# Attention scores and P @ v in causal blocks of 64 keys, on halves of the TensorE array

## The chip, the cores and the metric

The kernel runs on one core of a Trainium2 chip. The metric is the device time of one execution in microseconds (us). All data is float32.

## The reference, cut to what matters

```
x: [8, 256, 512]                                   # 8 sequences of 256 tokens
h = layernorm(x)
qkv = h @ w_qkv                                    # 32 q heads, 8 k and v heads, 128 wide
scores = q @ k.T * 128 ** -0.5                     # 4 q heads share a k and v head
scores += -slope[head] * sqrt(q_pos - k_pos)       # -inf where k_pos > q_pos
attn = softmax(scores);  o = attn @ v
x = x + o @ w_o
h = layernorm(x)
hits = softmax(h @ centroids.T / 0.1) > 0.01       # 64 clusters
dense = h @ weight.T + bias
x = x + where(any(hits, 1)[:, None] & any(hits, 0)[assignments], dense, 0)
```

## The kernel before

The eight sequences are taken in four pairs of two. A **unit** `u` is one k and v head with its four q heads, on one sequence: 8 heads x 8 sequences = 64 units, in order of pair, head, sequence. `slot` is the unit's number within its pair, 0 to 15; even units are the first sequence of a head, odd ones the second. The loop runs two units further to finish what is left.

Scores stand transposed: keys on the partitions, queries along the columns. With keys 0 to 127 all 256 queries are computed, with keys 128 to 255 the upper 128 queries only, so a unit has 4 x 256 + 4 x 128 = 1536 columns. What of them lies above the diagonal is masked by the bias (`dist` holds 3e38 there).

Several units are in work at once. In unit `u` these steps are issued, by an order written out by hand, each engine taking its own in that order:

- `scores(u, 0)` and `(u, 1)` (L376, two heads each) and, after a part of the projections, `(u, 2)` (L382, the second block of keys). VectorE multiplies and adds the bias (L378, L384).
- `over_keys(s[u], ..., max)`: VectorE's transposing reduces (L393 over 1024 columns, L394 over 512), and one small combine where both blocks hold the same queries (L396).
- `subtract_max(u - 1)`: GpSimd on the first block (L428), VectorE on the second (L431); then ScalarE's exp (L765).
- `attend(u - 2)`, named `av(0)` and `av(1)` in the order, for heads 0 and 1, then 2 and 3: TensorE's P @ v (L452, L453, into one bank of `p_acc`), VectorE's multiplication by 1 / sum into `oT` (L456). Then GpSimd's sums S1 to S4 of `oT` (L112 to L118).
- `over_keys(s[u - 1], ..., add)`, `over_quadrants`: TensorE transposes the reduced rows `r` (L403), VectorE reduces them (L407), and the result goes by DMA to HBM (L412) and back to all partitions (L421, `bc`): the maxima of `u` and 1 / sum of `u - 1`.
- `project_out(u - 2)`, steps named `w(1)` to `w(7)` (L474): product 1 reads `oT` of the first token tile, and begins with heads 0 and 1.
- the projections for later units: q (`qq`) in every unit, v (`e`) in slots 0, 1, 8, 9, k (`e`) in slots 3, 7, 11, 15 (L145), and the FFN (`f`) in slots 3 to 6 of the second and third pair.

All projections are by a scheme of seven products of quarter matrices (`strassen`), with sums of the weights on GpSimd or VectorE (`a_sums`: S1 to S4). In slots 0 and 8 VectorE makes S3 and S4 of the v weights after `subtract_max`.

TensorE's results lie in PSUM pools: `p_sc` has two banks, `p_acc` three; a new tile waits until the reader of an older one has released its bank. All loads stand on SP's queue. Before the loop, a warm-up has matmuls of `ones` on the whole array (L625), on halves of its rows (L628) and on halves of its columns (L631). Near the end, L933 and L938 compute the mask of the output columns; L938 uses 64 rows of the array.

The order of an even unit with a k or v projection:

```
qq(1), e(1), max_and_old(), e(2), f(0), av(0), e(6), exp_old(), av(1), more_sums(), f(1), rows_max(), f(1.5), e(7), qq(2)
```

and of an odd one:

```
e(1), qq(4), e(2), max_and_old(), f(0), e(6), av(0), exp_old(), e(7), av(1), f(1), f(1.5), e(5), qq(5)
f(2), norm(0), e(4), e(3), x(0), w(1), x(1), sum_old(), w(2, 5, 6), norm(1), qq(3)
```

Of the kernel before, what the change touches and what calls it, by code (L numbers as in the profile page):

```python
# [23 lines left out]
G = NH // NKV  # L24
# [11 lines left out]
X2_BUFS = 8  # L36

# [6 lines left out]
def sqrt_distances():  # L44


    k = np.arange(P)[:, None]
    q = np.arange(S)[None, :]
    d = np.where(q >= k, np.sqrt(np.maximum(q - k, 0).astype(np.float32)), np.float32(MASKED))
    return np.ascontiguousarray(d.astype(np.float32))  # L50
# [3 lines left out]
def block_kernel(  # L54
# [31 lines left out]
    alibi_hbm = [dram.tile([P, G * S], F32, tag=f"al_hbm{kv}", name=f"al_hbm{kv}", bufs=1) for kv in range(NKV)]  # L86
# [90 lines left out]
    def load_x2(t):  # L177
        x2[t] = work.tile([P, H], F32, tag="x2", name=f"x2_{t}", bufs=X2_BUFS)
        nc.sync.dma_start(x2[t], xf[ts(t, P), :])
# [69 lines left out]
    dist_sb = const.tile([P, S], F32, name="dist_sb")  # L249
# [97 lines left out]
    def alibi_bias(g):  # L347

        p, kv = divmod(g, NKV)
        t = bias_sb[g] = work.tile([P, G, S], F32, tag="alibi", name="alibi", bufs=2)  # L350
        if p == 0:
            for h in range(G):
                nc.gpsimd.tensor_scalar(t[:, h, :], dist_sb, -slopes[kv * G + h], None, ALU.mult)
            nc.sync.dma_start(alibi_hbm[kv], t.rearrange("p h q -> p (h q)"))
        else:
            nc.sync.dma_start(t.rearrange("p h q -> p (h q)"), alibi_hbm[kv])
# [3 lines left out]
    K0, K1 = G * S, G * P  # L360
    J0, J1 = K0 // 32, K1 // 32
    s_sb, inv_sb, bc_sb = {}, {}, {}

    def scores(u, i):
# [5 lines left out]
        if i == 0:  # L370
            s_sb[u] = work.tile([P, K0 + K1], F32, tag="s", name="s", bufs=3)
        s = s_sb[u]
        sc = p_sc.tile([P, 512], F32, tag="sc", name="sc")
        if i < 2:
            hh = 2 * i
            nc.tensor.matmul(sc, lhsT=kT[:, t0 : t0 + P], rhs=qT[:, hh : hh + 2, t0 : t0 + S],  # L376
                             start=True, stop=True)
            nc.vector.scalar_tensor_tensor(  # L378
                s[:, hh * S : (hh + 2) * S], sc, D ** -0.5,
                bias[:, hh : hh + 2, :].rearrange("p h q -> p (h q)"), ALU.mult, ALU.add)  # L380
        else:
            nc.tensor.matmul(sc, lhsT=kT[:, t0 + P : t0 + S], rhs=qT[:, :, t0 + P : t0 + S],  # L382
                             start=True, stop=True)
            nc.vector.scalar_tensor_tensor(  # L384
                s[:, K0:].rearrange("p (h q) -> p h q", h=G), sc.rearrange("p (h q) -> p h q", h=G),
                D ** -0.5, bias[:, :, :P], ALU.mult, ALU.add)

    def over_keys(s, r, which, op):  # L390
        a, b = which * J0, 2 * J0 + which * J1
        first, second = r[:, a : a + J0], r[:, b : b + J1]
        nc.vector.tensor_reduce(first, s[:, :K0].rearrange("p (j q) -> p j q", q=32), AX.X, op, apply_transpose=True)  # L393
        nc.vector.tensor_reduce(second, s[:, K0:].rearrange("p (j q) -> p j q", q=32), AX.X, op, apply_transpose=True)  # L394
        late = first.rearrange("p (h i) -> p h i", h=G)[:, :, 4:8]
        nc.vector.tensor_tensor(late, late, second.rearrange("p (h i) -> p h i", h=G), op)  # L396

    def over_quadrants(u, r, has_max, has_sum):

# [5 lines left out]
        for on, a, op in ((has_max, 0, ALU.max), (has_sum, J0, ALU.add)):  # L405
            if on:
                nc.vector.tensor_reduce(row[a : a + J0], tp[a : a + J0, :P].rearrange("j (c q) -> j q c", q=32),  # L407
                                        AX.X, op)
# [3 lines left out]
        nc.sync.dma_start(hbm[lo:hi], row[lo:hi])  # L412
        for on, i in ((has_max, 0), (has_sum, 1)):
            if on:

                if i == 0 or u == 0:
                    bc_sb[u] = work.tile([P, 2, G, S], F32, tag="bc", name="bc")
                to = bc_sb[min(u, NU - 1)][:, i if u < NU else 0]
                if i == 1:
                    inv_sb[u - 1] = to  # L420
                nc.sync.dma_start(to.rearrange("p h q -> p (h q)"),  # L421
                                  hbm[ts(i, J0)].rearrange("j q -> (j q)").partition_broadcast(P))

    def subtract_max(u, i):
        s, mx = s_sb[u], bc_sb[u][:, 0]
        if i == 0:
            k0 = s[:, :K0].rearrange("p (h q) -> p h q", h=G)
            gp(k0, k0, mx, sub)  # L428
        else:
            k1 = s[:, K0:].rearrange("p (h q) -> p h q", h=G)  # L430
            ve(k1, k1, mx[:, :, P:], sub)  # L431

    o_sb = {}

    def attend(u, e):
# [5 lines left out]
        i0 = bb * 2  # L441
        pT, inv = s_sb[u], inv_sb[u]
        if e == 0:
# [4 lines left out]
        oT = o_sb[u][0]  # L448
        hh = 2 * e
        av = p_acc.tile([P, 512], F32, tag="acc", name="av")  # L450
        av3 = av.rearrange("p (h q) -> p h q", h=2)
        nc.tensor.matmul(av, lhsT=v[:, i0, vc], rhs=pT[:, hh * S : (hh + 2) * S], start=True, stop=False)  # L452
        nc.tensor.matmul(av3[:, :, P:S], lhsT=v[:, i0 + 1, vc],  # L453
                         rhs=pT[:, K0 + hh * P : K0 + (hh + 2) * P].rearrange("p (h q) -> p h q", h=2),
                         start=False, stop=True)
# [552 lines left out]
```

## Time and profile before

| | |
|---|---|
| time, median of 3 runs | 1411.86 us (1409.46 to 1412.16) |
| the profiled execution | 1410.37 us, of which the profile's span is 1408.5 us |
| matmul records in it | 5875 |
| DMA over the span | 190.20 MB, mean 135 GB/s |

PE is TensorE's matmuls, PEld its weight loads, DVE VectorE, ACT ScalarE, POOL GpSimd, SP the engine whose queue issues the loads. Durations of one record and starts are from the profiled execution. A float32 matmul is two records, one per pass over the columns. A record's length goes on after the next has started, so a step is counted from start to start. In a row, `64*128` or `128*64` after the operation are the rows and columns of the array that it uses.

### The profile page before, as it was taken

What the parts mean: (1) busy time and instruction counts of PE and PEld (TensorE: products, weight loads), DVE (VectorE), ACT (ScalarE), POOL (GpSimd) and SP (SyncE); (2) the same over time, 40 slices, a digit from 0 to 9 for tenths busy, and PEclk for the clock granted to TensorE, in tenths of its full rate; (3) what the DMA queues carried; (4) which work ended last, traced back from release to release, by engine and by line L of the source; (5) the groups of instructions that cost most, each with busy time, mean ns of one, the idle gap of its engine ahead of it and who ended that gap; (6) DMA issues with size and microseconds to landing.
All of it is one profiled execution on the core that took longest, in us unless ns stands there. A gap on an engine that the chain in (4) does not pass through costs nothing.

```text
span 1408.5 us, 16598 instructions
## 1 busy us (share of the span) xinstructions
PE 1394.1 (99%) x5875; PEld 1085.8 (77%) x5875; DVE 923.3 (66%) x1724; ACT 370.3 (26%) x649; POOL 874.0 (62%) x878
## 2 busy tenths in 40 slices
PE   9999999999999999999999999999999999999997
PEld 7777777777878787777777787877787778787775
DVE  5557667676566665668656666566766566556877
ACT  2222222421232222242223222233122222222332
POOL 6387857776465654668656465565855666476562
PEclk9999999999999999999999999999999999999999
DMA  5334343343242544424334335344314352424343
GB/s 195 121 111 168 125 136 128 142 150 135 91 169 76 180 141 159 147 103 135 125 106 153 122 134 180 120 165 150 135 60 150 100 185 104 147 85 149 121 164 134
DMA packets 87312, 190.20 MB, mean 135 GB/s; under 512 B 11616, under 2 KB 20064, under 8 KB 87232
## 3 DMA queue, kind: packets, MB, share of 16 engines
q1 hardware_dynamic: 86464, 187.85, 38.4%
q10 hardware_dynamic: 720, 1.18, 0.2%
q8 instruction: 47, 0.77, 0.2%
q14 instruction: 33, 0.27, 0.1%
q0 software_dynamic: 48, 0.13, 0.0%
HBM read 176.03 MB, written 13.11 MB: 134 GB/s over the span
## 4 chain that ended last, share of the span: by engine, by line
PE 94%; DVE 3%; POOL 1%; DMA 1%; issue 1%; ACT 0%; SPq 0%; DVEq 0%; ACTq 0%; POOLq 0%
PE ps_oa L474 15%; PE ps_qa L145 15%; PE ps_qc L145 8%; PE sc L376 8%; PE ps_oc L474 8%; PE av L452 7%; PE sc L382 4%; PE ps_ka L145 4%; PE ps_ob L474 4%; PE av L453 4%; PE ps_va L145 4%; PE ps_qb L145 4%; PE ps_vc L145 2%; PE ps_kc L145 2%; PE ps_lg L520 2%; PE ps_f L520 2%
## 5 line engine op out<-in xcount | busy, mean ns | idle before, releaser
L506 POOL TENSOR_TENSOR x<-x,snap 128x256 f32<-128x256 f32 x189 | 134.3, 729 | 165.2 <-DVE x L500 119.5
L428 POOL TENSOR_TENSOR s<-s,bc 128x1024 f32<-128x1024 f32 x64 | 152.9, 2388 | 119.5 <-DMA bc<-row_hbm 119.4
L112 POOL TENSOR_TENSOR o_s<-oT 128x256 f32<-128x256 f32 x64 | 48.3, 755 | 196.2 <-DVE oT L456 196.2
L393 DVE TRANSPOSE_TENSOR_REDUCE r<-s 128x32 f32<-128x1024 f32 x128 | 157.9, 1234 | 5.5 <-ACT s L765 4.4
L161 ACT COPY qT<-ps_qa 128x512 f32<-128x512 f32 x128 | 74.7, 584 | 285.3 <-PE ps_qa L145 285.3
L489 ACT COPY snap<-ps_oa 128x256 f32<-128x256 f32 x189 | 70.4, 373 | 263.9 <-PE ps_oa L474 263.9
L474 PE MATMUL ps_oa<-wo,oT 128*128 128x256 f32 x512 | 132.4, 381 | 0.0
L765 ACT ACTIVATE s<-s 128x1536 f32<-128x1536 f32 x62 | 92.0, 1484 | 148.7 <-DVE s L431 124.8
L452 PE MATMUL av<-s,v 128*128 128x512 f32 x256 | 130.7, 592 | 0.0
L145 PE MATMUL ps_qa<-xT,wq 128*128 128x256 f32 x512 | 121.0, 379 | 0.0
L376 PE MATMUL sc<-qT,kT 128*128 128x512 f32 x256 | 120.4, 592 | 0.0
L145 PEld LDWEIGHTS ps_qa<-xT,wq 128*128 128x128 f32 x512 | 96.7, 190 | 26.4 <-issue 14.6
L378 DVE SCALAR_TENSOR_TENSOR s<-sc,alibi 128x512 f32<-128x512 f32 x128 | 87.7, 690 | 31.1 <-PE sc L376 30.6
L474 PEld LDWEIGHTS ps_oa<-wo,oT 128*128 128x128 f32 x512 | 91.4, 190 | 17.6 <-DVE oT L456 1.8
L384 DVE SCALAR_TENSOR_TENSOR s<-sc,alibi 128x512 f32<-128x512 f32 x64 | 44.3, 692 | 82.8 <-PE sc L382 82.8
L453 PEld LDWEIGHTS av<-s,v 128*128 128x128 f32 x256 | 48.6, 190 | 61.2 <-issue 61.2
L456 DVE TENSOR_TENSOR oT<-av,bc 128x512 f32<-128x512 f32 x128 | 84.0, 681 | 12.5 <-PE av L453 11.0
L394 DVE TRANSPOSE_TENSOR_REDUCE r<-s 128x16 f32<-128x512 f32 x128 | 85.6, 669 | 0.0
L500 DVE TENSOR_TENSOR x<-x,ps_oc 128x256 f32<-128x256 f32 x128 | 53.2, 416 | 37.1 <-PE ps_oc L474 36.3
L453 PE MATMUL av<-s,v 128*128 128x256 f32 x256 | 76.1, 379 | 0.0
L376 PEld LDWEIGHTS sc<-qT,kT 128*128 128x128 f32 x256 | 48.5, 190 | 34.1 <-issue 29.2
L396 DVE TENSOR_TENSOR r<-r 128x16 f32<-128x16 f32 x128 | 66.8, 522 | 4.4
(199 smaller groups left out, 2941.1 us busy)
## 6 DMA issues: line engine op xcount, KB each, us to landing
bc<-row_hbm SPq DMA_DIRECT2D x128, 512.0 KB, 4.7
wq<-in_w_qkv SPq DMA_DIRECT2D x32, 1024.0 KB, 8.2
wo<-in_w_o SPq DMA_DIRECT2D x32, 1024.0 KB, 7.7
alibi<-al_hbm SPq DMA_DIRECT2D x24, 512.0 KB, 8.7
wk<-in_w_qkv SPq DMA_DIRECT2D x16, 512.0 KB, 9.7
wv<-in_w_qkv SPq DMA_DIRECT2D x8, 1024.0 KB, 10.9
x<-in_x SPq DMA_DIRECT2D x16, 256.0 KB, 10.0
al_hbm<-alibi SPq DMA_DIRECT2D x8, 512.0 KB, 9.1
```

The lines of the kernel that those rows point to most:

```text
L145: nc.tensor.matmul(bank[:, cols], lhsT=lhsT, rhs=rhs, start=first and j == 0, stop=j == len(mms) - 1, skip_group_check=True)
L376: nc.tensor.matmul(sc, lhsT=kT[:, t0 : t0 + P], rhs=qT[:, hh : hh + 2, t0 : t0 + S], start=True, stop=True)
L378: nc.vector.scalar_tensor_tensor(s[:, hh * S : (hh + 2) * S], sc, D ** -0.5, bias[:, hh : hh + 2, :].rearrange("p h q -> p (h q)"), ALU.mu ...
L393: nc.vector.tensor_reduce(first, s[:, :K0].rearrange("p (j q) -> p j q", q=32), AX.X, op, apply_transpose=True)
L394: nc.vector.tensor_reduce(second, s[:, K0:].rearrange("p (j q) -> p j q", q=32), AX.X, op, apply_transpose=True)
L428: gp(k0, k0, mx, sub)
L452: nc.tensor.matmul(av, lhsT=v[:, i0, vc], rhs=pT[:, hh * S : (hh + 2) * S], start=True, stop=False)
L453: nc.tensor.matmul(av3[:, :, P:S], lhsT=v[:, i0 + 1, vc], rhs=pT[:, K0 + hh * P : K0 + (hh + 2) * P].rearrange("p (h q) -> p h q", h=2), s ...
L456: ve(oT[:, e].rearrange("p k m q -> p k (m q)"), av3, inv[:, hh : hh + 2, :], ALU.mult)
L474: nc.tensor.matmul(bank[:, :HH], lhsT=x[:, e, :], rhs=y[:, e, :], start=first and e == 0, stop=e == 1, skip_group_check=True)
L506: gp(c, c, s, ALU.add)
L765: nc.scalar.activation(s_sb[u - 1], s_sb[u - 1], AF.Exp)
```

## The change

Each sequence's 256 tokens are seen as four quarters of 64, and x is loaded so that they stand in the order 0, 1, 3, 2: the odd token tiles are loaded in two halves, swapped, and their output is stored the same way. The columns of a unit's scores are then:

- keys of quarters 0, 1 with queries of quarters 1, 3, 2: 4 x 192 columns (L399, two matmuls of 384 columns);
- the own keys of quarter 0 (partitions 0 to 63) and of quarter 2 (partitions 64 to 127), each with its own queries: 256 columns, by two matmuls of 64 output partitions each, on the two column halves of the array (L405);
- keys of quarters 3, 2 with queries of quarter 3: 256 columns (L409).

That makes 1280 columns. P @ v (L482) is five matmuls into two `p_acc` banks: the own keys of quarters 0 and 2 by two matmuls of 64 rows, on the row halves of the array, into a bank each (`attend(u - 2, 0)`, now ahead of the last score matmul); then 512 and 256 columns (`av(0)`), and 256 (`av(1)`). `av(0)` now gives the second token tile of all heads, `av(1)` the first. VectorE multiplies by 1 / sum in three instructions (L499 of 512 columns, L503 and L504 of 256), and GpSimd's S1 follows the first of them, S2 to S4 the others.

`over_keys` is one reduce over 1280 columns (L418), two combines (L423, and L424 on 64 partitions) and a memset of the combined part (L425). `subtract_max` has 1024 columns on GpSimd and 256 on VectorE (L466). The maxima come back by three DMAs instead of one. The bias tile has 1280 columns, and GpSimd makes it by eight instructions instead of four.

```
     def load_x2(t):
...
+        if t % 2:
+            for i in range(2):
+                nc.sync.dma_start(x2[t][ts(i, Q), :], xf[t * P + (1 - i) * Q : t * P + (2 - i) * Q, :])
...
+    AT_E, AT_D = G * 3 * Q, G * 4 * Q
     def scores(u, i):
...
         if i < 2:
-            hh = 2 * i
-            nc.tensor.matmul(sc, lhsT=kT[:, t0 : t0 + P], rhs=qT[:, hh : hh + 2, t0 : t0 + S],
+            n = 6 * Q
+            sc = p_sc.tile([P, 512], F32, tag="sc", name="sc")[:, :n]
+            nc.tensor.matmul(sc, lhsT=kT[:, quarters(t0, 0, 2)], rhs=qT[:, 2 * i : 2 * i + 2, quarters(t0, 1, 3)],
                              start=True, stop=True)
...
+        elif i == 2:
+            sc_late[0] = p_sc.tile([P, 512], F32, tag="sc", name="sc")
+            for half, at in ((slice(0, Q), 0), (slice(Q, P), 3)):
+                nc.tensor.matmul(sc_late[0][half, : G * Q], lhsT=kT[:, quarters(t0, at, 1)],
+                                 rhs=qT[:, :, quarters(t0, at, 1)], start=True, stop=True, skip_group_check=True)
         else:
-            nc.tensor.matmul(sc, lhsT=kT[:, t0 + P : t0 + S], rhs=qT[:, :, t0 + P : t0 + S],
-                             start=True, stop=True)
+            sc = sc_late[0]
+            nc.tensor.matmul(sc[:, G * Q :], lhsT=kT[:, quarters(t0, 2, 2)], rhs=qT[:, :, quarters(t0, 2, 1)],
+                             start=False, stop=True, skip_group_check=True)
+            nc.vector.scalar_tensor_tensor(s[:, AT_E:], sc, D ** -0.5, bias[:, AT_E:], ALU.mult, ALU.add)
...
     def over_keys(s, r, which, op):
-        nc.vector.tensor_reduce(first, s[:, :K0].rearrange("p (j q) -> p j q", q=32), AX.X, op, apply_transpose=True)
-        nc.vector.tensor_reduce(second, s[:, K0:].rearrange("p (j q) -> p j q", q=32), AX.X, op, apply_transpose=True)
-        nc.vector.tensor_tensor(late, late, second.rearrange("p (h i) -> p h i", h=G), op)
+        nc.vector.tensor_reduce(a, s.rearrange("p (j q) -> p j q", q=32), AX.X, op, apply_transpose=True)
+        nc.vector.tensor_tensor(first[:, :, QT : 2 * QT], first[:, :, QT : 2 * QT], heads(rest), op)
+        nc.vector.tensor_tensor(first[Q:, :, 2 * QT :], first[Q:, :, 2 * QT :], heads(own[Q:]), op)
+        nc.vector.memset(own[Q:], -MASKED if op == ALU.max else 0.0)
...
+                    nc.sync.dma_start(to[:, :AT_E], flat(hbm[:e]).partition_broadcast(P))
+                    nc.sync.dma_start(to[:Q, AT_E:], flat(hbm[e:J0]).partition_broadcast(Q))
+                    nc.sync.dma_start(
+                        to[Q:, AT_E:].rearrange("p (h q) -> p h q", h=G),
+                        flat(hbm[:e]).rearrange("(h j) -> h j", h=G)[:, 2 * Q :].partition_broadcast(Q))
...
+    def attend(u, i):
...
+        if i == 0:
+            a, b = av_sb[u] = [p_acc.tile([P, 512], F32, tag="acc", name="av") for _ in range(2)]
+            mm(a[:, : G * Q], v[:Q, i0, vc], pT[:Q, AT_E:AT_D], True, False)
+            mm(heads(b)[:, :, Q:], v[Q:, i0 + 1, vc], heads(pT[Q:, AT_E:AT_D]), True, False)
+            return
...
+        if i == 1:
+            mm(heads(b), v[:, i0, vc], first[:, :, Q:], False, False)
+            mm(heads(b)[:, :, :Q], v[:, i0 + 1, vc], heads(pT[:, AT_D:]), False, True)
+            ve(out[:, :, 1, :], heads(b), inv_first[:, :, Q:], ALU.mult)
+            a_sums(gp, o_sb[u][1], "S1")
+        else:
+            mm(a[:, G * Q :], v[:, i0, vc], first[:, :, :Q], False, True)
+            ve(out[:, :, 0, :Q], heads(a[:, : G * Q]), heads(inv[:, AT_E:]), ALU.mult)
+            ve(out[:, :, 0, Q:], heads(a[:, G * Q :]), inv_first[:, :, :Q], ALU.mult)
+            a_sums(gp, o_sb[u][1], "S2 S3 S4")
...
         def max_and_old():
             scores(u, 2)
+            if u > 1:
+                attend(u - 2, 0)
+            scores(u, 3)
             over_keys(s_sb[u], r, 0, ALU.max)
```

## The prediction

> **What bounds the kernel now.** I read the page first: busy times, then the chain that ended last.
>
> ```profile
> PE 1394.1 (99%) x5875; PEld 1085.8 (77%) x5875; DVE 923.3 (66%) x1724; ACT 370.3 (26%) x649; POOL 874.0 (62%) x878
> PE 94%; DVE 3%; POOL 1%; DMA 1%; issue 1%; ACT 0%; SPq 0%; DVEq 0%; ACTq 0%; POOLq 0%
> ```
>
> TensorE (PE) is busy 99% of the span and is 94% of the chain. But matmul ends are modelled, so I went to the steps from start to start, in the timeline of TensorE for one unit (start, length, line, operation):
>
> ```profile
> 712.87 1.88 PE L376 MATMUL sc<-qT,kT 128*128 128x512 f32 x4
> 714.59 1.03 PE L145 MATMUL ps_va<-wv,xT 128*128 128x256 f32 x4
> 715.45 1.89 PE L145 MATMUL ps_qa<-xT_t,wq 128*128 128x256 f32 x8
> 717.18 1.03 PE L145 MATMUL ps_vb<-wv,xT 128*128 128x256 f32 x4
> 718.04 1.02 PE L382 MATMUL sc<-qT,kT 128*128 128x512 f32 x2
> 718.90 1.03 PE L145 MATMUL ps_va<-e_t,xT_t 128*128 128x256 f32 x4
> 719.76 1.02 PE L452 MATMUL av<-s,v 128*128 128x512 f32 x2
> 720.62 0.59 PE L453 MATMUL av<-s,v 128*128 128x256 f32 x2
> ```
>
> Each float32 matmul is two records. A record of 512 columns steps 0.429 us (1.72 / 4), one of 256 columns 0.216 (0.86 / 4), with no gap anywhere: 0.834 ns a column and 2 ns. What leaves TensorE's queue shortens the kernel one for one, and what makes TensorE wait lengthens it one for one. The waits view has under 7 us of waits of PE itself in the whole run, nearly all at the two ends.
>
> **The columns.** One unit before: scores 6 records of 512 (4 of L376, 2 of L382), P @ v 4 of 512 (L452) and 4 of 256 (L453): 10 x 0.429 + 4 x 0.216 = 5.155 us. After: scores 4 records of 384 (0.3225 by the slope), two matmuls of 256 on column halves, 2 records of 256; P @ v two matmuls of 256 on row halves, then 2 records of 512 and 4 of 256. If each pair of halves costs as much as one matmul, that is 1.290 + 0.438 + 0.432 + 0.438 + 0.858 + 0.863 = 4.319 us: 0.836 less, and over 64 units **-53.5 us**.
>
> **Do halves run side by side?** The warm-up does just that on 128 columns, in the rows of its lines and the first transposes:
>
> ```profile
> 3.87 1.65 PE L628 MATMUL tpx<-ones 64*128 64x128 f32 x12
> 5.45 0.92 PE L631 MATMUL tpx<-ones 128*64 128x128 f32 x12
> 6.31 1.09 PE L296 MATMUL tpx<-ident,xn 128*128 128x128 f32 x8
> ```
>
> Twelve records of column halves take 0.92 us, eight of the whole array 1.09: the starts come in pairs 6 ns apart, a pair per 0.109 us, which is the step of one whole record. Row halves also start in pairs 6 ns apart, a pair per 0.213, the step the whole array had just before (it was still at half its pace). So I count a pair as one matmul and 6 ns per pass (the 0.438 above).
>
> **What the array pays to change shape.** The best row is the tail, where L938 uses 64 rows, L520 follows without any wait, and steps have the pace of the main part:
>
> ```profile
> 1389.01 0.59 PE L938 MATMUL rsel<-onehot,csel 64*128 64x512 f32 x1
> 1389.53 0.70 PE L520 MATMUL ps_f<-w_ffn,xnT_bc 128*128 128x512 f32 x1
> ...
> 1390.06 0.59 PE L520 MATMUL ps_f<-w_ffn,xnT_bc 128*128 128x512 f32 x1
> ```
>
> From L938's last record to L520's first is 0.519 instead of 0.429 (+90 ns), and from that to the next 0.533 (+104 ns): its weights could not be loaded ahead. Row halves to whole array costs 0.194. Into column halves, the first pair of L631 takes 0.207 instead of 0.109, so 0.090 + 0.098 = 0.188; into row halves the whole load again, 0.195. The rows that speak for more: whole to row halves in the warm-up +0.300 (at half pace), row to column halves 0.348 - 0.213 + 0.098 = 0.233. For less: L631's second weight load starts 59 ns after the first, so column weights may hide to 59. The new order of a unit is whole, column pair (L405), row pair (L482), whole: three changes, 0.577 us (0.45 to 0.70). 62 units have three, the first two and last two units two: 35.8 + 1.5 = **+37.3 us**. Net of busy time: **-16.2**.
>
> The Trainium skill ("TensorEngine Tiling (Array Packing)", Key Properties) says that changing the tiling mode drains the array; it has no price, and its table's "up to 2x" for a dimension of 64 alone would give the full -53.5. The skill ("TensorE: Matmul & The Clock Gate", LDWEIGHTS) puts a weight load at columns / 1.2 ns, 107 for 128 and 53 for 64: the tail's 104 agrees, the warm-up's 98 for column halves does not, and by the page the three changes would be 45 ns a unit, 2.9 us in all, cheaper.
>
> **New waits of TensorE for VectorE.** P @ v shrinks from 2.59 us to 1.73 behind the last score matmul, but what VectorE (DVE) must do until then hardly shrinks. Its queue in a unit without a k or v projection (slot 13):
>
> ```profile
> 635.81 0.69 DVE L384 SCALAR_TENSOR_TENSOR s<-sc,alibi 128x512 f32<-128x512 f32 x1 [1.89 <-PE sc L382]
> 636.42 1.23 DVE L393 TRANSPOSE_TENSOR_REDUCE r<-s 128x32 f32<-128x1024 f32 x1
> 637.58 0.67 DVE L394 TRANSPOSE_TENSOR_REDUCE r<-s 128x16 f32<-128x512 f32 x1
> 638.28 0.18 DVE L396 TENSOR_TENSOR r<-r 128x16 f32<-128x16 f32 x1
> 638.37 0.69 DVE L431 TENSOR_TENSOR s<-s,bc 128x512 f32<-128x512 f32 x1
> 638.97 1.28 DVE L456 TENSOR_TENSOR oT<-av,bc 128x512 f32<-128x512 f32 x2
> 639.92 1.09 PE L474 MATMUL ps_oa<-wo,oT 128*128 128x256 f32 x4
> L396 DVE TENSOR_TENSOR r<-r x128: 174/277/2171, 30.5 to 1356.5; 128x16 f32<-128x16 f32 x128
> ```
>
> Call the end of the last score matmul T (635.61 here). The output projection's first product (L474) starts at T + 4.31 and needs only the first L456 (its heads 0 and 1), done at T + 4.05. After the change, steps by the same rows: multiply-add T + 0.20, +0.61; one reduce of 1280 columns 1.53 (the 1024 one's slope, and 34 ns to the dependent); two small combines 0.09 and 0.21, a memset 0.08; subtraction of 256 columns 0.34; the multiply of 512 columns 0.60; two of 256, 0.34 and 0.42: T + 4.42. The first product now needs token half 0 of all heads, so all of it, and 0.16 more for the semaphore and the weight load (0.056 + 0.107, as at 640.31): T + 4.58, while TensorE is there at 1.29 + 0.43 + 1.73 = T + 3.45. A wait of 1.1 us in odd units that have no k or v and no FFN: slots 13 of four pairs and 5 of two, **+6.6**.
>
> In slots 0 and 8 (seven units) VectorE also makes S3 and S4 of wv (0.60 each) in that stretch. S3 ends at T + 3.75, its product (e 7) is due at T + 3.45; the add of ps_vb, whose bank the next product takes, ends at T + 4.69: together 0.5 a unit, **+3.5**. The two accumulator banks that P @ v now holds from before the last score matmul are no wait elsewhere: the built order gives the next tiles the third bank or the one freed by the 512-column multiply (T + 3.7, wanted at T + 4.3 in odd units with k or v); even units without them reach the projection at T + 5.2.
>
> A combine takes 176 ns free and up to 2171 while GpSimd (POOL) runs: in the sums it averages about 0.87. The second combine may pay that again; for the sums there are 1.0 to 1.7 us before the transpose of r (L403) is due, for the maxima GpSimd is mostly idle. I put **+1.0**, 0 to 36.
>
> **The rest.** Three broadcasts of the maxima instead of one: same 512 KB, two more issues on SP (0.45 each), one with 256-byte runs; GpSimd's subtraction waits for them, with 0.7 us or more before exp needs it: nothing while that holds; every other load behind them moves by 0.9 against landings of 8 us and a unit of lead. exp is 1280 columns instead of 1536, on an engine busy 26%. First bias tile: eight GpSimd instructions instead of four, 0.9 us on the path to wq's sums, for which TensorE already waits 0.2 at 16.2 us; two more x loads ahead of wk lie beside it: **+0.9**. Split stores: one more issue at the end, **+0.5**.
>
> Sum: -16.2 + 6.6 + 3.5 + 1.0 + 0.9 + 0.5 = -3.7. The profiled execution took 1410.37 (span 1408.5), 0.1% under the median of 1411.86; so 1406.7 by the one, 1408.2 by the other: I say **1407**. A measurement of this kernel tells about 0.2% from no change, 2.8 us.
>
> **Rivals.**
> - *As summed*, 1400 to 1414: chance 0.40 (faster 0.27, same 0.09, slower 0.04).
> - *A change of shape costs more*, so it is slower. From 0.214 us each the waits (12.5 us) and changes eat all 53.5. At the 0.233 of the warm-up's row to column step: 43.3 + 1.9 + 12.5 - 53.5 = +4, 1416; at 0.30, 1428. For it: every warm-up change was dearer than the tail's; against: they were at half pace. 0.26 (same 0.06, slower 0.20).
> - *Changes are cheaper*, 0.15 each (column weights hidden, drain 70): 28.5 + 12.5 - 53.5 = -12.5, 1399; without the new waits too, down to 1386. 0.18, all faster.
> - *VectorE becomes the bound of the stretch*: the maxima's two combines are held by GpSimd as the sums' are, 1.4 us in 13 units and 0.9 in the 20 odd ones with k or v: +36, 1443; half of it 1425. 0.10, slower.
> - *The halves run one after the other* (the warm-up's pairs read the same data; here two streams differ): +0.86 us a unit, +55, 1462. 0.06, slower.
>
> Faster 0.45, same 0.15, slower 0.40. The range 1393 to 1425 leaves out the last rival, half of VectorE's, the dearest changes and the cheapest end: 0.2.
>
> **What would show it.** Steps right: pairs of L405 and L482 starting 6 ns apart with 0.216 to the next pass; about 0.19 of extra step at each of three places in a unit; ps_oa waiting for DVE oT about 1.1 us in six units and the v projection for wv in seven; no such waits in odd units with k or v. Wrong: pairs that step 0.43, extra steps over 0.21 (slower) or near 0.1 (clearly faster), TensorE waiting for av's banks or for r, or GpSimd's subtraction ending after VectorE's.

## The result: 1.7% slower

The changed kernel takes 1435.35 us (median of 4 runs, 1432.86 to 1437.27), the kernel before 1411.36 beside it (4 runs): a ratio of 1.0171, 95% interval 1.0152 to 1.0190. The profiled execution took 1435.0 us, its span is 1433.0, 24.5 longer than before.

The two lines of the page that answer to those of before:

```profile
PE 1386.0 (97%) x6259; PEld 1088.9 (76%) x6259; DVE 924.6 (65%) x1916; ACT 356.5 (25%) x649; POOL 882.0 (62%) x910
PE 80%; DVE 10%; DMA 4%; ACT 2%; issue 2%; SPq 1%; DVEq 0%; POOL 0%; ACTq 0%
```

TensorE has less to do, but it is only 80% of the chain that ended last; VectorE now has 10% of it and DMA 4%. So TensorE is made to wait. The waits view names whom (total, times, longest, in us; before, nearly all of 7 us of waits were at the ends):

```profile
PE ps_oa L523 <- DVE oT L504: 19.0, 20, 2.6
PE ps_va L155 <- DVE wv L126: 3.9, 7, 0.7
PE tpx L311 <- ACT xT L312: 3.1, 3, 1.2
```

L523 is the output projection and L504 VectorE's last multiply into `oT`. The prediction had six such waits; there are twenty.

The halves themselves did what was expected. TensorE's timeline in one unit without waits (slot 1):

```profile
732.17 1.03 PE L155 MATMUL ps_vb<-wv,xT 128*128 128x256 f32 x4
733.13 0.65 PE L405 MATMUL sc<-qT,kT 128*64 128x256 f32 x4
733.71 0.70 PE L482 MATMUL av<-s,v 64*128 64x256 f32 x4
734.34 0.70 PE L409 MATMUL sc<-qT,kT 128*128 128x256 f32 x2
734.88 1.03 PE L155 MATMUL ps_va<-e_t,xT_t 128*128 128x256 f32 x4
```

Four half records of L405 or L482 (two matmuls, two passes) take 0.58 and 0.63 us to the next group where two whole ones take 0.43: each pair starts 5 to 8 ns apart and steps like one record, and the rest is the change of shape.

Length of the unit, after minus before, from first score matmul to first score matmul, by slot (us):

| pair | 0 | 1 | 2 | 3 | 4 | 5 | 6 | 7 | 8 | 9 | 10 | 11 | 12 | 13 | 14 | 15 |
|---|---|---|---|---|---|---|---|---|---|---|---|---|---|---|---|---|
| 1st | .22 | .24 | 2.21 | -.30 | 1.61 | 2.53 | .71 | -.30 | .49 | -.30 | -.18 | .13 | 2.00 | 1.01 | .30 | -.30 |
| 2nd | -.53 | -.30 | .55 | -.30 | -.06 | -.30 | -.30 | -.30 | .48 | -.30 | .63 | .12 | .73 | 1.01 | .30 | -.30 |
| 3rd | .48 | -.30 | -.06 | -.30 | -.30 | -.30 | -.30 | -.30 | .65 | -.30 | -.30 | .13 | 1.13 | 1.01 | .30 | -.30 |
| 4th | .49 | -.30 | -.25 | -.30 | 1.14 | 1.01 | -.30 | -.30 | -.27 | -.30 | -.08 | -.30 | .03 | 1.02 | 1.65 | |

Where nothing waits, a unit is exactly 0.30 us shorter. Over 63 units that would be 18.9 us less; the sum of the table is 15.1 more. So about 34 us of new waits stand in the loop, 23 of them in even slots. The rest of the loss is outside the table: the first score matmul starts 3.7 us later (28.0 instead of 24.3), from the last unit's first score matmul to the last matmul it takes 2.1 us longer, and from the last matmul's start to the end of the span 11.5 us instead of 7.9.

**Two things that hold VectorE.** In an even unit without k or v (slot 2 of the second pair) VectorE's timeline reads (start, length; in brackets the idle time before and its releaser):

```profile
408.93 1.51 DVE L418 TRANSPOSE_TENSOR_REDUCE r<-s 128x40 f32<-128x1280 f32 x1
410.48 0.64 DVE L423 TENSOR_TENSOR r<-r 128x8 f32<-128x8 f32 x1
...
411.45 0.43 DVE L466 TENSOR_TENSOR s<-s,bc 128x256 f32<-128x256 f32 x1
412.52 0.69 DVE L499 TENSOR_TENSOR oT<-av,bc 128x512 f32<-128x512 f32 x1 [0.65 <-DMA bc<-row_hbm]
```

L499 is the first multiply by 1 / sum, and it waits for the DMA that brings 1 / sum. SP's timeline shows what stands ahead of that DMA (L451):

```profile
403.98 0.33 SPq L454 DMA_DIRECT2D bc<-row_hbm  x1
404.36 0.45 SPq L455 DMA_DIRECT2D bc<-row_hbm  x1
404.86 0.61 SPq L456 DMA_DIRECT2D bc<-row_hbm  x1
405.51 0.60 SPq L451 DMA_DIRECT2D bc<-row_hbm  x1
```

Before the change the two broadcasts stood together:

```profile
390.98 0.83 SPq L421 DMA_DIRECT2D bc<-row_hbm  x2
```

So 1 / sum is issued 1.53 us after the first broadcast instead of 0.36 (the second of the two issues before starts at 391.34), and then takes longer to land: 6.2 us from issue to landing instead of 5.1 (medians). From the landing of the row's store to the landing of 1 / sum the median is 7.8 us, and was 5.6. 18 times a multiply starts within 0.15 us of that landing (before: 2).

The other one is seen in slot 14 of the second pair, first on VectorE, then on GpSimd:

```profile
670.13 1.12 DVE L423 TENSOR_TENSOR r<-r 128x8 f32<-128x8 f32 x1
```

```profile
668.88 2.35 POOL L463 TENSOR_TENSOR s<-s,bc 128x1024 f32<-128x1024 f32 x1
```

The combine of eight columns lasts until GpSimd's subtraction of 1024 ends (671.25 and 671.23). This is no accident: of the 256 combines 77 took over 0.5 us, and every one of them ends 21 to 28 ns behind the end of a GpSimd instruction; the 132 that no GpSimd instruction overlaps took at most 0.17 us. Most of the 77 belong to the sums; 15 are combines of the maxima, all behind GpSimd's subtraction.

The hold itself is not new. Before the change, too, 15 combines of the maxima (L396) took over 0.5 us and up to 2.2, all behind that subtraction (L428). From the end of the maxima's reduce to VectorE's subtraction (L466) the 61 units from 2 to 62 take 50 us together, 25 before; without a hold a unit takes 0.54 us, 0.13 before. So the hold makes 17 us in both kernels, and the 25 us more are the second combine and the memset. What is new is that TensorE now waits behind it.

The Trainium skill ("SBUF — State Buffer", Who interferes with whom) says that a VectorE instruction with two inputs in SBUF and a GpSimd instruction that reads SBUF exclude each other for the whole instruction. These rows agree with it.

### The profile page after: what moved, and what is told of

The parts are those of the page before. It is cut to its first block, busy times and chain, and to the rows that moved or that the text cites. A ratio compares the mean times of both kernels' runs of the same rounds, so it can differ in the third digit from the quotient of the medians.

```text
span 1433.0 us, 17986 instructions
## 1 busy us (share of the span) xinstructions
PE 1386.0 (97%) x6259; PEld 1088.9 (76%) x6259; DVE 924.6 (65%) x1916; ACT 356.5 (25%) x649; POOL 882.0 (62%) x910
## 4 chain that ended last, share of the span: by engine, by line
PE 80%; DVE 10%; DMA 4%; ACT 2%; issue 2%; SPq 1%; DVEq 0%; POOL 0%; ACTq 0%
PE ps_oa L523 15%; PE ps_qa L155 13%; PE ps_oc L523 7%; PE av L482 6%; PE ps_qc L155 6%; PE sc L399 5%; PE ps_ob L523 4%; PE ps_ka L155 4%; PE ps_va L155 3%; DMA bc<-row_hbm 3%; DVE r L418 3%; PE sc L409 3%; PE sc L405 2%; PE ps_qb L155 2%; PE ps_vc L155 2%; PE ps_kc L155 2%
## 5 line engine op out<-in xcount | busy, mean ns | idle before, releaser
L418 DVE TRANSPOSE_TENSOR_REDUCE r<-s 128x40 f32<-128x1280 f32 x128 | 192.7, 1506 | 5.1 <-ACT s L817 2.2
L482 PE MATMUL av<-s,v 64*128 64x256 f32 (+2 forms) x640 | 170.8, 442 | 0.0
L523 PE MATMUL ps_oa<-wo,oT 128*128 128x256 f32 x512 | 134.2, 385 | 19.5 <-DVE oT L504 19.0
L411 DVE SCALAR_TENSOR_TENSOR s<-sc,alibi 128x512 f32<-128x512 f32 x64 | 44.3, 692 | 145.7 <-PE sc L409 145.7
L482 PEld LDWEIGHTS av<-s,v 128*128 128x128 f32 (+1 forms) x640 | 91.4, 188 | 61.7 <-issue 55.4
L523 PEld LDWEIGHTS ps_oa<-wo,oT 128*128 128x128 f32 x512 | 90.5, 190 | 43.0 <-DVE oT L504 28.0
L817 ACT ACTIVATE s<-s 128x1280 f32<-128x1280 f32 x62 | 78.8, 1271 | 163.5 <-DVE s L466 161.9
L399 PE MATMUL sc<-qT,kT 128*128 128x384 f32 x256 | 93.1, 486 | 0.0
L401 DVE SCALAR_TENSOR_TENSOR s<-sc,alibi 128x384 f32<-128x384 f32 x128 | 69.7, 555 | 16.6 <-PE sc L399 12.4
L549 DVE TENSOR_TENSOR x<-x,ps_oc 128x256 f32<-128x256 f32 x128 | 53.5, 418 | 33.8 <-PE ps_oc L523 32.9
L523 PE MATMUL ps_oa<-wo_t,oT 128*128 128x256 f32 x256 | 65.8, 380 | 0.0
L523 PE MATMUL ps_oc<-wo_t,o_s 128*128 128x256 f32 x256 | 65.7, 379 | 0.0
L523 PE MATMUL ps_ob<-wo,oT 128*128 128x256 f32 x256 | 65.7, 379 | 0.0
L523 PE MATMUL ps_oc<-wo,o_s 128*128 128x256 f32 x256 | 65.7, 379 | 0.0
L523 PE MATMUL ps_oa<-wo_t,o_s 128*128 128x256 f32 x256 | 65.7, 379 | 0.0
```

The lines of the kernel that those rows point to most:

```text
L399: nc.tensor.matmul(sc, lhsT=kT[:, quarters(t0, 0, 2)], rhs=qT[:, 2 * i : 2 * i + 2, quarters(t0, 1, 3)], start=True, stop=True)
L401: nc.vector.scalar_tensor_tensor(s[:, ts(i, n)], sc, D ** -0.5, bias[:, ts(i, n)], ALU.mult, ALU.add)
L418: nc.vector.tensor_reduce(a, s.rearrange("p (j q) -> p j q", q=32), AX.X, op, apply_transpose=True)
L482: mm = lambda out, lhsT, rhs, start, stop: nc.tensor.matmul(out, lhsT=lhsT, rhs=rhs, start=start, stop=stop, skip_group_check=True)
L523: nc.tensor.matmul(bank[:, :HH], lhsT=x[:, e, :], rhs=y[:, e, :], start=first and e == 0, stop=e == 1, skip_group_check=True)
L549: nc.vector.tensor_add(c, c, ps[5][:, :HH])
```

## The experiments

All ratios are to the kernel before, run on the same chip. In the sets of runs below the kernel before took 1410.0 to 1411.0 us, 1411.4 beside the changed kernel, so one or two us between times of different sets say nothing; the ratios allow for it. The first theory (A) was that the late 1 / sum makes the even units wait; its rivals were VectorE's own queue, later called C when the held combines were seen, and changes of shape dearer than the trace shows.

**1. One broadcast of the maxima**

```
-    nc.sync.dma_start(to[:, :AT_E], flat(hbm[:e]).partition_broadcast(P))
-    nc.sync.dma_start(to[:Q, AT_E:], flat(hbm[e:J0]).partition_broadcast(Q))
-    nc.sync.dma_start(to[Q:, AT_E:]..., flat(hbm[:e])...[:, 2 * Q :].partition_broadcast(Q))
+    nc.sync.dma_start(to, flat(hbm[:J0]).partition_broadcast(P))
...
-    gp(s[:, :AT_D], s[:, :AT_D], mx, sub)
+    gp(s[:, :AT_E], s[:, :AT_E], mx[:, :AT_E], sub)
+    gp(s[:Q, AT_E:AT_D], s[:Q, AT_E:AT_D], mx[:Q, AT_E:], sub)
+    gp(own, own, heads(mx[Q:, :AT_E])[:, :, 2 * Q :], sub)        # own = heads(s[Q:, AT_E:AT_D])
```

> The maxima come back by one DMA of 512 KB to all partitions, as before the change, instead of three; GpSimd subtracts them in three pieces (768 columns on all partitions, 256 on each half), so everything is computed as in the changed kernel. Theory A: in even units without k or v the wait of TensorE for oT (about 13 us over 14 units) comes from 1 / sum, whose broadcast stands behind the three on SP's queue and lands 7.8 us after the row's store instead of 5.6, so that VectorE's first multiply (L499) waits for it. Then it lands after 5.6 to 6 us again, the waits for oT fall from 19.0 us to 7 to 9, and the time falls by 8 to 13 us, to 1422 to 1427. Rival B: VectorE's own queue is what is long, or GpSimd holds it; then the landing moves and the time doesn't (within 2 us of 1435), or it grows by GpSimd's extra 0.85 us a unit where exp waits for it.

Measured: 1430.97 us, ratio 1.0147 (1.0130 to 1.0164). 1 / sum lands after 5.7 us again, and two multiplies start at the landing, as before the change (18 in the changed kernel). The waits for `oT` fall from 19.0 us (20) to 13.2 (13), the time by about 4. Unit by unit the loop is 5.2 us shorter. A is true of the transfer, and not enough for the time: in the same units the combines still hold VectorE.

**2. x in its own order**

```
-        if t % 2:
-            for i in range(2):
-                nc.sync.dma_start(x2[t][ts(i, Q), :], xf[t * P + (1 - i) * Q : t * P + (2 - i) * Q, :])
+        nc.sync.dma_start(x2[t], xf[ts(t, P), :])
...
-            nc.tensor.transpose(tp[:, ts(c, P)], xn[:, ts(c, P)], ident)
+            nc.tensor.transpose(tp[:, ts(c, P)], xn[:, ts(c, P)], ident if by is None else by)   # by: halves swapped
...
-            ve(out[:, :, 1, :], heads(b), inv_first[:, :, Q:], ALU.mult)
+            ve(out[:, :, 1, Q:], heads(b)[:, :, :Q], inv_first[:, :, Q : 2 * Q], ALU.mult)
+            ve(out[:, :, 1, :Q], heads(b)[:, :, Q:], inv_first[:, :, 2 * Q :], ALU.mult)
```

> x is loaded and stored whole, in its own order; the order of quarters is made by the transposes (a swapped identity for odd tiles), and VectorE writes the second token tile of oT back in its own order by two multiplies of 256 columns instead of one of 512. Everything is computed. Theory: the split loads make the start 3.7 us later and the split stores the end 3.6 us later. Then the first score matmul is at 24.3 to 25 us instead of 28.0, the end 7.5 to 8 us after the last matmul instead of 11.15, and the time falls by 7 us less the 0.16 us that VectorE's extra multiply costs in the 20 units where TensorE waits for oT (3 us): about 1431, 1428 if that is hidden. Rival: the start is late because of something else that the change does there (the bias tile's eight instructions on GpSimd); then only the end moves, 1431 to 1435.

Measured: 1433.78 us, ratio 1.0163 (1.0147 to 1.0178). The end is as short as before the change (7.9 us from the last matmul's start instead of 11.5), the start is not (28.5 us): TensorE hardly waits for x's second tile there (0.2 us), but 2.0 us for wk's DMA and 2.0 for GpSimd's sums of wq, which stand behind the bias tile's eight instructions; behind the second of these waits its granted clock is 0.50 for 3.4 us. The rival held for the start, the theory for the end.

**3. First token tile first**

```
         if i == 1:
+            mm(a[:, G * Q :], v[:, i0, vc], first[:, :, :Q], False, True)
+            ve(out[:, :, 0, :Q], ...), ve(out[:, :, 0, Q:], ...)
         else:
+            mm(heads(b), ...), mm(heads(b)[:, :, :Q], ...)
+            ve(out[:, :, 1, :], heads(b), inv_first[:, :, Q:], ALU.mult)
+            a_sums(gp, o_sb[u][1])
```

> The first token tile of P @ v and its two multiplies go ahead of the second tile's (512 and 256 columns) and its multiply, so the output projection's first product waits for two multiplies of 256 columns instead of all three; GpSimd's S1 comes after the last multiply. Everything is computed. Theory: the first product waits for VectorE's queue, which is shorter by the multiply of 512 columns (0.60 us): the six waits in odd units fall from 1.26 to 0.65 us, those of even units by 0.6 each or to nothing: 9 to 12 us less, 1423 to 1426. Rival: GpSimd's S1 becomes late for product 5 (its start moves by about 0.6 us, with 1.7 us of products 1 and 2 ahead of it); then half or more of that comes back as waits of ps_oc for POOL, 1430 or more.

Measured: 1442.57 us, ratio 1.0230 (1.0211 to 1.0249): 7 us slower. By the steps the waits for `oT` did fall by 6.7 us, five of the six odd ones to 0.67 (0.65 expected). But TensorE waits 4.6 us more for `r` before its transposes, 1.7 more for ScalarE's copies of xT and 3.7 in 13 k steps for copies of kT, all behind the same queues; the combines of the maxima are held for longer too (62 us from reduce to L466, 50 before). S1 was not the only thing that became late, so the rival named the right sign and too narrow a reason. Which of these came first stays open. The profiled run is also the slowest of the four, 1447.37 us at a mean clock of 0.991 (the others 0.994 to 0.996): four of its waits in the loop, of 1.8 to 2.1 us, are each followed by 3.4 us at a granted clock of 0.50, which the changed kernel's loop never has. So the sums from this trace explain more than the 7 us of the median.

**4. No halves**

```
-            for half, at in ((slice(0, Q), 0), (slice(Q, P), 3)):
-                nc.tensor.matmul(sc_late[0][half, : G * Q], lhsT=kT[:, quarters(t0, at, 1)], rhs=qT[:, :, quarters(t0, at, 1)], ...)
+            nc.tensor.matmul(sc_late[0][:, : G * Q], lhsT=kT[:, quarters(t0, 0, 2)], rhs=qT[:, :, quarters(t0, 0, 1)], ...)
...
-            mm(a[:, : G * Q], v[:Q, i0, vc], pT[:Q, AT_E:AT_D], True, False)
-            mm(heads(b)[:, :, Q:], v[Q:, i0 + 1, vc], heads(pT[Q:, AT_E:AT_D]), True, False)
+            mm(a[:, : G * Q], v[:, i0, vc], pT[:, AT_E:AT_D], True, False)
```

> Each pair of matmuls on halves of the array is replaced by one on the whole array with as many columns; the own keys of quarter 2 are left out of the scores and of P @ v thereby (it is not the reference). What remains is the change without any change of shape. Theory A: the pairs cost what a whole matmul costs plus 0.52 us a unit for three changes of shape, which is 33 us over the run; but TensorE comes to the output projection 0.52 us sooner against the broadcast of 1 / sum, and the waits of some 14 to 18 units grow by that: 23 to 26 us less, 1409 to 1412. Rival: the waits in even units are VectorE's own, which counts from the last score matmul and moves with it: then the full 33 us, 1402. Rival: the halves cost little (the pair's excess is hidden): under 10 us less.

Measured: 1413.57 us, ratio 1.0019 (1.0008 to 1.0030), 22 us less than the changed kernel. 28 of the 63 units are shorter by 0.54 to 0.56 us than in the changed kernel, which makes the 21 that wait for nothing 0.85 shorter than before the change: 0.55 is the price of the three changes of shape with their pairs, 0.85 the columns' gain without it. Over 64 units it would be 35 us. The waits for `oT` grew to 24.0 us in 25 units, as theory A said they must when TensorE comes sooner and VectorE does not; two of them are followed by 3.4 us at half the clock. **Even with the changes of shape free, this kernel would not be faster than the one before**: the waits, with what follows them, and the two ends take all of the gain.

**5. Late combines**

```
     def over_keys(s, r, which, op):
         nc.vector.tensor_reduce(a, s.rearrange("p (j q) -> p j q", q=32), AX.X, op, apply_transpose=True)
+        if op == ALU.max:
+            late_max.append((a, op))          # L423 to L425 of these come behind av(1)
+        else:
+            combine(a, op)
```

> The changed kernel with the two combines and the memset of the maxima (L423 to L425) moved behind VectorE's multiplies of oT, where nothing waits for them until the transpose of r; all is computed. In the changed kernel's even units without k or v they take 0.7 to 2.7 us while GpSimd subtracts, instead of 0.4. Theory A (the late broadcast of 1 / sum alone): the multiply then waits for the broadcast all the same; only the six odd waits shrink by 0.38 us each and slots 12 and 14 a little: 2 to 4 us less, 1431 to 1433. Theory C (the combines held by GpSimd alone are what makes even units wait): 10 to 13 us less, 1422 to 1425.

Measured: 1433.13 us, ratio 1.0166 (1.0149 to 1.0183), 2 us less (0.7 by the ratios), which the intervals can't tell from nothing; in the traces the loop is 6.7 us shorter. The waits for `oT` are 10.4 us in 15 units; 19 multiplies now start at the landing of 1 / sum. In the last two units the transpose of `r` comes right behind the combines and now waits for them, up to 4.4 us, which takes 3 us and more back.

**6. Both**

The edits of 1 and 5 together.

> One broadcast of the maxima and the late combines together; all is computed. Theory A+C (both hold VectorE in the same units, the later one counts): the even units' waits are nearly all gone, waits of TensorE for oT fall from 19.0 to 4 to 6 us (the six odd units at 0.9 each), and the time is 1418 to 1424, which is more than the sum of the two edits alone. Rival: something else is late in even units (GpSimd's subtraction and exp): 1428 to 1431, as with one broadcast alone.

Measured: 1417.51 us, ratio 1.0047 (1.0030 to 1.0064): 18 us less, where the two alone gave 4 and 2 (by the ratios 17.5, 3.4 and 0.7). From its waits view:

```profile
PE tp_r L445 <- DVE r L433: 8.0, 8, 2.4
PE ps_oa L533 <- DVE oT L514: 3.0, 7, 0.5
```

The waits for `oT` are down to 3.0 us, the six odd ones (0.61 by the steps) and one more; 40 of the 63 units now have the full -0.30, where 26 had it. Either of the two holds VectorE in the even units, and each hides the other: a single repair shows little. What it left is the transposes of `r`, 5.0 of the 8.0 us in the last units and 2.2 in the first pair.

**7. Bias parts on ScalarE**

```
-                nc.gpsimd.tensor_scalar(t[:, AT_E:]..., dist_sb[:, 3 * Q :]..., slope, None, ALU.mult)
+            nc.scalar.activation(t[:, AT_E:]..., dist_sb[:, 3 * Q :]..., AF.Copy, scale=-slopes[g * G + h])
```

> In the first pair, where the bias tiles are made, ScalarE makes the own-key parts of each (4 instructions on 128 columns) and GpSimd only its four of 192 columns, 2.8 us instead of 4.9 a tile; all is computed. The first pair lost 10 us against the kernel before where the three others lost 1 to 3. Theory: half of that is GpSimd's four more instructions a tile, which push its subtraction and with it exp and VectorE's combines: 4 to 6 us less, 1429 to 1431. Rival: the first pair's waits are the same as the others' (broadcast and combines) and GpSimd has room: within 1.5 us of 1435.

Measured: 1432.58 us, ratio 1.0160 (1.0144 to 1.0176), 2.8 us less, with intervals that overlap. Between the two, and nearer to the rival: the first pair's units gained 1.3 us in this profile; its start was unchanged (28.0), being held by x's second tile there. GpSimd's extra instructions are at most a small part of the first pair's loss of 10 us.

**8. All repairs at once**

Edits 1, 2, 5, 7, S3 of the v weights a unit earlier, and in the odd order for slots 5 and 13 without FFN:

```
-            ..., e(5), qq(5)
-            f(2), ..., w(1), x(1), sum_old(), w(2, 5, 6), norm(1), qq(3)
+            ..., e(5), qq(5), qq(3)
+            f(2), ..., w(1), x(1), sum_old(), w(2, 5, 6), norm(1)
```

> The halves stay; every loss named so far is repaired: x in its own order (second experiment), one broadcast of the maxima, late combines, bias parts on ScalarE, S3 of the v weights made a unit earlier, and in slots 5 and 13 of pairs without FFN product 3 of q ahead of the output projection. All is computed. If the losses are those, they add up to 13 (even units) + 6 (odd) + 4 (wv) + 3.5 (end) + 2 to 4 (start) + 4 (first pair) less 1 to 2 for what GpSimd and VectorE do more: 1402 to 1408, below the kernel before. If they stand in for each other: 1410 to 1418.

Measured: 1423.43 us, ratio 1.0095 (1.0080 to 1.0110), slower than 6. The units of slots 5 and 13 are 2.4 to 3.8 us longer than in 6, and nothing else is by more than 1: product 3 adds into the bank of product 5, so it waits until VectorE has added product 5, behind the multiplies of `oT`. The new order put a wait of 2.05 us in place of one of 0.61. And product 3 no longer stands ahead of the transpose of `r`, which now waits 0.96 us for VectorE (slot 13 of the first pair).

**9. The repairs that held**

Edits 1, 2, 5 (not in the first and the last two units) and 7; product 3 back in its place, and for the six odd units:

```
-            e(1), qq(4), e(2), max_and_old(), f(0), e(6), av(0), ...
+            bare = slot in (5, 13) and t_ffn is None
+            e(1), bare or qq(4), e(2), max_and_old(), bare and qq(4)
+            f(0), e(6), av(0), ...
```

> x in its own order, one broadcast of the maxima, late combines (but not in the first and the last two units, where the transpose of r comes right behind them), bias parts on ScalarE; product 3 of q back in its place, and in slots 5 and 13 of pairs without FFN the q step of L155 that stood ahead of the last score matmuls put behind them instead. All is computed. From the sixth experiment's 1417.5: the end 3.5 less (whole stores), the start 3 less, the last units' transposes 4 to 5 less, the six odd waits of 0.61 us less 3.5, and 0 to 2 more for VectorE's extra multiply and a wait for a score bank in those units: 1403 to 1407, faster than the kernel before by 0.3 to 0.5%. If the last units' waits have another cause than the order of combines: 1408 to 1410, no difference.

Measured: **1399.28 us**, ratio 0.9926 (0.9913 to 0.9940): 0.7% faster than the kernel before, and 4 us below the range that was expected. The page's two lines and the waits for `oT`:

```profile
PE 1379.1 (99%) x6259; PEld 1089.2 (78%) x6259; DVE 908.7 (65%) x1982; ACT 361.5 (26%) x681; POOL 925.8 (66%) x1006
PE 91%; DVE 4%; DMA 2%; POOL 1%; issue 1%; ACT 0%; SPq 0%; DVEq 0%; ACTq 0%; POOLq 0%
```

```profile
PE ps_oa L538 <- DVE oT L519: 0.4, 2, 0.2
```

All six odd units have -0.29 now, the first score matmul is at 24.8 us, the end 7.9 us behind the last matmul's start, as before the change. Some of these edits (bias on ScalarE, late combines) could help the kernel before as well; that was not tried, but it had only 7 us of waits to give.

**10. A fourth change of shape**

```
             scores(u, 2)
+            scores(u, 3)
             if u > 1:
                 attend(u - 2, 0)
-            scores(u, 3)
```

> The changed kernel with the last score matmul (L409) between the column pair and the row pair instead of behind both: whole, column, whole, row, whole, four changes of the array's shape a unit instead of three; all is computed. By the steps of the changed kernel's trace (into columns 0.093 + 0.044, into rows 0.093 + 0.098, back to whole 0.090 + 0.104) a unit costs 0.194 us more, 12 us over the run; the last score matmul ends 0.63 us sooner against VectorE's chain, so the six odd waits and a few even ones shrink by up to that: 8 to 12 us more, 1443 to 1447. Rival: changes of shape are cheap and the 0.5 us a unit is something else of the halves (the pair itself): no more than 3 us more.

Measured: 1435.27 us, ratio 1.0176 (1.0160 to 1.0191): no more than the changed kernel. The price is there: 19 units are longer by 0.20 us and seven by 0.15, as the steps said. But 19 others, most of them units that wait for VectorE, are 0.2 to 0.6 us shorter, since the last score matmul ends sooner, and the two nearly cancel; the loop of this trace is 2.3 us longer, with two stretches at half the clock in it. The expectation had the price right and the give-back too small. The rival's number (no more than 3 us) came true, but not for its reason: the price shows wherever nothing waits.

## Why the prediction was wrong, by its own steps

Predicted 1407 us with 1393 to 1425; measured 1435.35, beyond the range. The steps are from start to start in the two traces.

| step of the sum | predicted | measured |
|---|---|---|
| columns, pairs side by side | -53.5 | -52.6 (-54.3, and 256 pairs at 6.5 ns) |
| changes of shape | +37.3 | +33.5 |
| six odd units | +6.6 | +7.6 |
| wv's S3 and S4 | +3.5 | +3.5 (5.1 less 1.6 before) |
| other waits for `oT`: even units without k or v | 0 | +14.7 (1.5 of it in slot 5 of the first pair) |
| combines held by GpSimd | +1.0 | in the rows above |
| start | +0.9 | +3.7 |
| end | +0.5 | +3.6 |
| second transposes of x in slot 12 | 0 | +3.1 |
| rest (steps right behind a wait 2.0, k steps 1.3, behind the last unit's start about 2, small ones) | 0 | +7.4 |

*Right: columns and halves.* The net of busy time was put at -16.2 us; it is -19.1. The pairs start 5 to 8 ns apart, and a unit without waits is 0.30 us shorter where 0.26 was predicted. The three changes cost 93 + 44, 93 + 98 and 90 + 104 ns, 0.52 together (0.577 predicted): column weights are partly hidden, the rest is what the tail's row had shown. Experiment 4 has the same from the other side, 0.55 with the pairs. The rivals on dearer changes (0.214 and more each) and on halves one after the other are refuted; a change cost 0.174, halfway to the rival with 0.15, whose 1399 would still have needed all waits but the summed ones to stay away. The Trainium skill ("TensorEngine Tiling (Array Packing)", Key Properties) has the drain; the runs put its price at 0.09 us a change, and at 0.17 with the weights that cannot be loaded ahead.

*Right: odd units and wv.* In slot 13 TensorE was at the output projection at T + 3.45, as worked out, and VectorE's last multiply ended at T + 4.66 where T + 4.42 was predicted:

```profile
653.41 0.68 DVE L499 TENSOR_TENSOR oT<-av,bc 128x512 f32<-128x512 f32 x1
...
654.34 0.41 DVE L504 TENSOR_TENSOR oT<-av,bc 128x256 f32<-128x256 f32 x1
```

*Wrong: "even units without them reach the projection at T + 5.2".* This is the step that failed. TensorE does reach it then; the step set this against VectorE's chain of an odd unit, T + 4.58, and called the rest slack. But that chain was taken from slot 13, where 1 / sum has long landed and GpSimd is idle. In the fifteen even units that wait, VectorE's last multiply ended at T + 5.2 to T + 8.1, and the waits for `oT` beyond the six odd ones cost 14.7 us where none was summed. In even units both operands were already near the edge before the change: in slots 2, 4, 6, 10, 12 and 14 the multiply mostly started 1.2 to 1.8 us after the landing of 1 / sum, and the combine of the maxima took up to 2.2 us instead of 0.17. What hid that was slack of 2.0 us: TensorE came to the projection at T + 6.0 and needed only the first multiply, done at T + 4.05. Now it comes at T + 5.2 and needs the last one, done at T + 4.66 at the earliest, which leaves 0.5; and 1 / sum lands 2.2 us later.

*Wrong: "Three broadcasts of the maxima instead of one: ... nothing while that holds".* The step asked who waits for the maxima, and moved "every other load behind them" by 0.9 us against a unit of lead. The next one behind them is the broadcast of 1 / sum, whose lead was 1.7 us in even units and not a unit. It lands 2.2 us later: 1.2 from the issues (1.5 us from the first to its own, instead of 0.36) and 1.1 because it is under way for longer (6.2 us instead of 5.1). Why that is so was not tested; with one broadcast ahead of it (experiment 1) it is back at 5.3.

*Half right: "for the maxima GpSimd is mostly idle. I put +1.0, 0 to 36".* That is so in odd units, where the combines took 0.17 us each. In even units GpSimd subtracts just then, and did before the change: the row of L396 with its 2171 ns mixes sums and maxima, and its longest are maxima. The rival "VectorE becomes the bound of the stretch" named this mechanism, at 0.10, in 13 waiting units and 20 odd ones with k or v, at 1.4 and 0.9 us each; almost none of those odd ones waits for VectorE (slots 1, 3, 7, 9 and 15 have their -0.30, but for unit 1; slot 11's 0.4 is a wait for ScalarE's copy of kT), its place was the even units.

*Mis-sized: start and end.* The start was put down to the bias tile, 0.9 us. It was 3.7: first the split loads (x's second tile lands in two halves, wk's DMA is issued at 4.20 us instead of 2.58), and when these are whole, still the bias tile and wq's sums behind it (experiment 2). By the steps the waits are 1.8 us longer, small gains take 0.5 back, and 2.4 us are steps at half the pace, while the granted clock is 0.50 behind the first of them (8.1 to 14.9 us). With both repaired the first score matmul is at 24.6 and 24.8 us (experiments 8 and 9), and the clock there stays whole. At the end a half store is not half a store: the issues themselves became long. SP's store issues before the change (least, median, most in ns), and its last ones in the changed kernel and in experiment 9, where the 2.03 us hold two issues of 0.33 and the time between them:

```profile
L957 SPq DMA_DIRECT2D out<-x x7: 332/333/351, 1393.5 to 1404.2; - x7
```

```profile
1425.12 1.39 SPq L1009 DMA_DIRECT2D out<-x  x1
1426.61 3.19 SPq L1007 DMA_DIRECT2D out<-x  x2
```

```profile
1391.38 2.03 SPq L1029 DMA_DIRECT2D out<-x  x2
```

One issue of a whole tile took 0.33 us before the change, with 14 stores on SP's and ScalarE's queues; with 24 in the changed kernel, most of them of 64 partitions, the last ones took 1.4 to 1.7.

*Not foreseen:* slot 12, where exp waits for VectorE's subtraction (L466), which stands behind a held combine, and then for a table load of 1.28 us; ScalarE's copy of xT behind it makes the next transposes wait, 1.1 to 1.4 us in three units.

## What to carry to other kernels

Slack belongs to a place, not to a kernel: before calling a wait hidden, take the chain from the very unit in which it would end last, here the even units, and ask of each operand when it arrived. When a transfer is split, price it by what stands next on the same queue, not by its own reader. And when one repair gives little, ask whether two things release the same instruction: removing either showed 4 and 2 us, removing both 18.

## What the runs showed of the hardware

- A combine of VectorE with both inputs in SBUF stood still until GpSimd's running instruction was done: 77 of 77 long ones ended 21 to 28 ns behind a GpSimd end, up to 2.3 us for 8 columns. The reduce of 1280 columns, with one input, took its usual 1.51 us while GpSimd subtracted (slot 14 above).
- At a change of the array's shape the step into the new shape was 90 to 93 ns longer, and the next one by 98 ns for row halves, 104 for the whole array and 44 for column halves (256 columns a matmul). The first weight load of a new shape starts with its matmul (both at 734.34 us in the unit of slot 1 above), where the load for the next matmul in the same shape starts 0.22 us ahead of it (734.66 for 734.88).
- After a wait of about 2 us TensorE may come back at half its pace. In experiment 8 a wait of 1.93 us was followed by ten records at twice their step. The window view of that stretch, with busy time, (records) and granted clock:

```profile
126.00:130.00 4.00, 4.00 (x19) 1.00 0.94 299
132.70:136.60 3.90, 3.85 (x10) 0.57 1.04 380
136.90:140.00 3.10, 3.07 (x15) 1.00 0.05 15
```

  Of six waits of that length in this kernel (idle 1.89 to 1.93 us) two had this after-effect; their ten steps are 2.0 us longer together, and their units 1.4 us longer than the other four. Behind the first score matmul, the traces of all kernels here have 27 waits with 1.7 to 2.7 us of idle time: 11 were followed by 3.41 us at a granted clock of 0.50, and 16 were not, among them the changed kernel's own of 1.80, 2.24 and 2.63 us. What decides between them was not tested. At the start of the changed kernel it goes with the 2.64 us wait for x's second tile (the granted clock is 0.50 from 8.1 to 14.9 us). The Trainium skill ("TensorE: Matmul & The Clock Gate", Part 1) gives about 3.4 us of idling for that; these runs had it after less.
